# Two-row groups with 16-byte gaps for the input of a convolution stage, and transfers that begin at even rows

## The chip, the core and the metric

The kernel runs on one NeuronCore of one Trainium2 chip. Each compute engine (TensorE, called PE in the profile; VectorE, DVE; ScalarE, ACT; GpSimd, POOL) runs its own instruction stream in order. Transfers between memory and the on-chip buffer are issued from a further queue, SyncE (SP), and are carried out by 16 DMA engines that all issuers share. The metric is the time of one execution on the device in microseconds (us). Three runs of the kernel before gave 2673.44, 2696.38 and 2699.72 us, with a median of 2696.38.

## What is computed

The input `x` has 16 images of 16 channels of 256 x 256 float32 values. Two layers follow each other, each of the form "normalise in groups of two channels, convolve, add".

```python
def _gn(v, G=8, eps=1e-5):
    g = v.reshape(B_, G, C_ // G, H_, W_)
    m = jnp.mean(g, axis=(2, 3, 4), keepdims=True)
    s = jnp.var(g, axis=(2, 3, 4), keepdims=True)
    return ((g - m) / jnp.sqrt(s + eps)).reshape(v.shape)
# layer 0: a circular 3x3 convolution over 16 channels, written with FFTs
x = x + _L0_conv_ref(_gn(x), L0_conv_weight)
# layer 1: a Laplace-type spectral operator with poles and residues
x = x + _L1_conv_ref(_gn(x), L1_conv_ty, L1_conv_tx, L1_conv_weights_pole1,
                     L1_conv_weights_pole2, L1_conv_weights_residue)
```

Layer 0 needs the mean and the variance of every group of `x` before an image can be convolved. It is computed as a direct 3x3 convolution on PE. Layer 1 is computed with matrix products that stand for Fourier transforms.

## The kernel before

The program has four stages in time. The first (lines 100 to 701, from 0 to about 594 us) loads `x`, convolves it and stores the result `v` into the scratch tensors `vD`; beside this it builds tables for layer 1. The other three transform `v`, mix the channels per mode, and transform back. The change touches the first stage alone.

**How x lies.** The host prepares `x` as an array of shape (16 images, 128 partitions, 34 rows, 258 columns). A partition holds one channel and one of eight interleaved sets of rows, with a column of halo on either side, so a row is 258 x 4 = 1032 bytes and the 34 rows of a partition follow each other without a gap. Of the 34 rows, the first half-tile uses rows 0 to 17 and the second rows 16 to 33.

**How x is loaded.** A half-tile `xt` has 18 rows on 128 partitions; there are five buffers of them (line 109). `load_part` (line 122) issues one DMA for some of the rows of a half, and `PARTS` (line 120) cuts the 18 rows into 5, 4, 5 and 4. So a half takes four DMAs, an image eight, and the stage 128. A DMA of 5 rows moves one piece of 5160 bytes for each partition, a DMA of 4 rows one piece of 4128 bytes. All go through SP's queue. The eight DMAs of image 0 are issued first of all (line 131), then 12 constants, then image 1. From there `load_part` is called inside the main loop (line 686), for the image two ahead, at steps 4, 5, 10, 11 and 16, 17, 22, 23 of the 24 steps of an image.

**Who reads it.** DVE takes moments of row pairs of each half (`moments`, line 177): its call `j` reads rows 1+2j and 2+2j of the half. The calls for image b stand in the loop 36 to 29 steps ahead of its convolution for the first half, and from 21 to 18 steps ahead for the second. A handful of small operations then give the image's scaled weights `wc`. In `conv` (line 280) each of the 24 steps of an image issues 16 small matrix products, of 32 rows by 32 columns, which run on quarters of the PE array; each is recorded as two matmuls, with a weight load before each. So a step is 32 matmuls and 32 weight loads.

**What follows the product.** Every six steps a unit is complete. ACT moves four PSUM banks into the tiles `pair` (three buffers) and `far` (line 313); DVE adds the two and sums them (line 261); POOL subtracts (line 264); ACT squares for the statistics of layer 1 (line 272). Two DMAs of 512 KB then store `pair` into `vD` (line 323), in pieces of 2048 bytes, from SP's queue. A buffer of `pair` is free again when its store has landed. Table building (`make_hat`, `make_c`) puts further DMAs into SP's queue, among them 20 broadcasts `s_h<-hD` of 256 KB.

**What sets the order.** The stage is scheduled by hand (line 118): the loop at line 675 decides at which step each piece is issued, and each engine and queue runs its pieces in that order. At most eight of SP's DMAs are under way at a time, since SP's DMAs use eight semaphores in turn and a DMA waits until the last one on its semaphore has landed.

Of the kernel before, what the change touches and what calls it, by code (L numbers as in the profile page):

```python
# [18 lines left out]
N = 256  # L19
P = 128  # L20
# [4 lines left out]
def conv_then_laplace_kernel(ctx: ExitStack, tc: tile.TileContext, a: dict, out: bass.AP):  # L25
# [15 lines left out]
    nc = tc.nc  # L41
    x = a["x"]
# [66 lines left out]
    xp = p1.enter_context(tc.tile_pool(name="xt", bufs=5))  # L109
# [7 lines left out]
    psu = p1.enter_context(tc.tile_pool(name="p_setup", bufs=1, space=PSUM))  # L117
    p1.enter_context(tc.manual_schedule())

    PARTS = 0, 5, 9, 14, 18  # L120

    def load_part(t, b, h, i, j):
        nc.sync.dma_start(out=t[:, i:j], in_=x[b][:, 16 * h + i : 16 * h + j])

    def load_x(b, h):
        t = xp.tile([P, 18, N + 2], FP, name="xt", tag="xt")
        for i, j in zip(PARTS, PARTS[1:]):
            load_part(t, b, h, i, j)
        return t
# [545 lines left out]
    for g in range(24 * B + 3):  # L675
        conv(g)
        if g - 24 * (B - 4) in (16, 19, 22, 27, 30, 33):
            next(early, None)
        b, n = divmod(g, 24)
        if b + 2 < B and n % 12 in (4, 5, 10, 11):  # L680
            h, k = n // 12, (4, 5, 10, 11).index(n % 12)
            if k == 0:
                halves.setdefault(b + 2, []).append(
                    xp.tile([P, 18, N + 2], FP, name="xt", tag="xt")
                )
            load_part(halves[b + 2][h], b + 2, h, PARTS[k], PARTS[k + 1])
        for b, gen in at_step.get(g, ()):
            going.append([b, gen, next(gen)])
        for it in list(going):
            while it[2] is not None and g >= 24 * it[0] - it[2][0]:  # L690
                it[2][1]()
                it[2] = next(it[1], None)
            if it[2] is None:
                going.remove(it)
        run_jobs(g, slots.get(n, ()))
        next(tables, None)
# [31 lines left out]
    m, n = cols[:, 16:17], cols[:, 17:18]  # L728
# [136 lines left out]
    for u in range(len(units) + 1):  # L865
        at = units[u] if u < len(units) else None
        if at is not None:
            now = vq
            t = lp.tile([P, 2, 4, 3, P], FP, name="t", tag="t")
# [8 lines left out]
        if last is not None:  # L878
            i, b0 = last[:2]
# [9 lines left out]
        if last is not None:  # L889
            first_slots(b0, spec, *done)  # L890
            if b0 == B - 4:
                project(i, psd)
                (nc.sync if i + 1 < C else nc.scalar).dma_start(
                    out=aD[:, 2 * i : 2 * i + 2].rearrange("p r n -> p (r n)"),
                    in_=spec.rearrange("p r f b -> p (r f b)"),
# [504 lines left out]
    for n, (k, b0) in enumerate(units):  # L1400
# [13 lines left out]
        r = rp.tile([P, 4, 2, N], FP, name="r", tag="r")  # L1414
# [105 lines left out]
def _laid_out(x, L0_conv_weight, L1_conv_ty, L1_conv_tx, L1_conv_weights_pole1, L1_conv_weights_pole2, L1_conv_weights_residue):  # L1520

    g = {"ty": np.asarray(L1_conv_ty), "tx": np.asarray(L1_conv_tx)}
    x = np.asarray(x)
    xp = np.concatenate([x[..., -1:], x, x[..., :1]], -1)

    rows = 64 * np.arange(2)[:, None, None] + 2 * np.arange(33) - 1 + np.arange(2)[:, None]

    rows = np.concatenate([np.pad(rows, ((0, 0), (0, 0), (1, 0))), np.pad(N - 1 - rows, ((0, 0), (0, 0), (0, 1)))])
    g["x"] = xp[:, :, rows % N].transpose(0, 2, 3, 1, 4, 5).reshape(-1, P, 34, N + 2)
    w = np.asarray(L0_conv_weight)  # L1530
    band = np.zeros((4, 2, C, 2, 3, 2, C), w.dtype)
    for r in range(4):
        for j in range(2):
            for phase in range(2):
                for yo in range(2):

                    dy = (j - 1 - yo + 2 * phase) * (1 if r < 2 else -1)
                    if abs(dy) <= 1:
                        band[r, j, :, phase, :, yo, :] = w[:, :, 1 - dy, :].transpose(1, 2, 0)
    g["wband"] = band.reshape(P, 2, 3, 32)  # L1540

    def pairs(z):
        z = np.ascontiguousarray(z)
        return z.view(np.float32).reshape(z.shape + (2,))

    p1, p2, rs = (
        pairs(np.asarray(z))
        for z in (L1_conv_weights_pole1, L1_conv_weights_pole2, L1_conv_weights_residue)
    )

    g["poles"] = np.stack([p1.reshape(P, 8, 2), p2.reshape(P, 8, 2)], 1).transpose(0, 3, 1, 2).reshape(P, 2, 16)

    g["res_kq"] = np.repeat(rs.transpose(1, 3, 0, 2, 4).reshape(64, C, 4, 2), 2, 0)

    g["res_ip"] = np.repeat(rs.transpose(0, 2, 1, 3, 4).reshape(64, C, 4, 2), 2, 0)
    g["pole1_ip"] = np.repeat(p1.transpose(0, 2, 1, 3).reshape(64, C, 2), 2, 0)

    z = p2.reshape(4, 4, 8, 2, 4, 2).transpose(3, 1, 4, 0, 2, 5)
    z = np.broadcast_to(z[:, None, :, :, None], (2, 2, 4, 4, 2, 4, 8, 2))
    g["pole2_k"] = z.reshape(P, 32, 2)  # L1560

    e1 = p1.transpose(0, 2, 1, 3).reshape(4, 16, C, 2)
    g["pole_e1"] = np.stack([e1, e1], 1).reshape(P, C, 2)
    g["pole_e2"] = np.repeat(p2.transpose(0, 2, 1, 3).reshape(64, C, 2), 2, 0)
    return {n: np.ascontiguousarray(v) for n, v in g.items()}
# [17 lines left out]
```

## Time and profile before

| What | Value |
|---|---|
| median of three runs | 2696.38 us (2673.44 to 2699.72) |
| time of the profiled execution | 2673.52 us |
| its span, first to last instruction | 2671.8 us |
| mean granted TensorE clock | 0.980 |
| PE busy | 2494.0 us (93% of the span) |
| DVE busy | 1977.7 us (74%) |
| ACT busy | 1446.7 us (54%) |
| POOL busy | 1327.2 us (50%) |
| DMA traffic | 653.11 MB, mean 244 GB/s |

The span splits by stages as follows. The first row is the time until the first product of the convolution starts, and the second is the rest of the first stage.

| Stretch (us) | Length | PE busy | DVE busy | ACT busy | DMA share |
|---|---|---|---|---|---|
| 0 to 28.7 | 28.7 | 1.8 | 16.0 | 1.5 | 0.87 |
| 28.7 to 594 | 565.3 | 506.8 | 407.8 | 328.5 | 0.77 |
| 594 to 1245 | 651.0 | 625.1 | 540.7 | 381.2 | 0.57 |
| 1245 to 1910 | 665.0 | 622.4 | 510.2 | 414.0 | 0.74 |
| 1910 to 2671.8 | 761.8 | 737.9 | 503.0 | 321.5 | 0.81 |

"Busy" is the time in which an engine executed something. Matmuls are pipelined and their ends are modelled, so that a stretch of PE that looks busy may still run below PE's best rate. The DMA share is the mean over the 16 DMA engines of the time in which they carried a packet; a packet is one contiguous piece, and the records of the trace give its size, its start and its duration. "Issue" as a reason for a wait means that the engine waited for nothing that the profile shows.

### The profile page before, as it was taken

The page shows a single profiled execution, that of the slowest core. Times are in us where ns is not written, and L with a number is a line of the kernel's source. Part 1 is how long each engine was busy: PE and PEld are TensorE (multiplying, and loading weights), DVE is VectorE, ACT ScalarE, POOL GpSimd, SP SyncE. Part 2 cuts the span into 40 slices and gives each one's busy share as a digit, 9 for nine tenths or more (in the row PEclk, how much of TensorE's full clock was granted, in tenths as well). Part 3 has the DMA queues.
Part 4 walks back from the last instruction along what each step waited for, and adds up shares of the span by engine and source line. Part 5 has one row for each costly group of instructions (what it writes and reads, how often), then busy time and mean ns, then how long its engine had stood idle before and what let it go on. Part 6 is the DMA issues. An engine that isn't in the chain of part 4 may idle for free.

```text
span 2671.8 us, 83862 instructions
## 1 busy us (share of the span) xinstructions
PE 2494.0 (93%) x35314; PEld 1879.1 (70%) x35314; DVE 1977.7 (74%) x3805; ACT 1446.7 (54%) x2726; POOL 1327.2 (50%) x1180
## 2 busy tenths in 40 slices
PE   5988899888999999997999999999799999999998
PEld 2544454456777777774877888887688888888887
DVE  7767778738888888886877877887267666766666
ACT  2555666575666666664666666666344444444443
POOL 1333368432333333333366656676456566565653
PEclk9999999999999999997999999999899999999999
DMA  7787778855566556554777777777788888888884
GB/s 273 266 283 268 266 240 289 283 176 192 190 252 235 202 195 253 230 204 160 222 221 221 230 231 219 220 232 218 218 318 290 284 294 288 284 291 282 301 285 169
DMA packets 290871, 653.11 MB, mean 244 GB/s; under 512 B 44566, under 2 KB 159382, under 8 KB 280640
## 3 DMA queue, kind: packets, MB, share of 16 engines
q1 hardware_dynamic: 289456, 640.55, 71.1%
q8 instruction: 278, 4.55, 0.7%
q0 software_dynamic: 896, 3.02, 0.4%
q10 hardware_dynamic: 144, 4.19, 0.4%
q14 instruction: 97, 0.79, 0.1%
HBM read 368.15 MB, written 280.36 MB: 243 GB/s over the span
## 4 chain that ended last, share of the span: by engine, by line
PE 62%; DMA 5%; DVE 3%; SPq 3%; POOL 1%; ACT 1%; issue 1%; DVEq 0%; ACTq 0%; POOLq 0%
PE ps_mix L1096 9%; PE ps_y L764 9%; PE ps_p L1337 9%; PE ps_y L772 8%; PE ps_f L1361 8%; PE ps_f L1362 8%; PE ps_x L807 4%; DMA yD<-yt 4%; PE ps_s L1014 3%; PE ps_h L1321 2%; SPq L1110 2%; DVE sg L1030 2%; PE psd L792 1%; SPq L1083 1%; ACT yt L1209 1%
## 5 line engine op out<-in xcount | busy, mean ns | idle before, releaser
L1096 PE MATMUL ps_mix<-abd,sg 128*64 128x128 f32 x8192 | 484.3, 276 | 35.2 <-ACT yt L1209 22.2
L1096 PEld LDWEIGHTS ps_mix<-abd,sg 128*64 128x64 f32 x8192 | 450.5, 138 | 91.8 <-ACT yt L1209 49.6
L294 PE MATMUL ps_conv<-xt,wc 32*32 32x512 f32 x12288 | 451.9, 615 | 55.6 <-issue 49.2
L1301 POOL TENSOR_TENSOR u<-yk 128x512 f32<-128x512 f32 (+1 forms) x268 | 353.2, 1351 | 281.1 <-PE ps_p L1337 215.6
L294 PEld LDWEIGHTS ps_conv<-xt,wc 32*32 32x32 f32 x12288 | 251.2, 104 | 246.2 <-issue 163.5
L780 ACT ACTIVATE t<-ps_y,vmr 128x384 f32<-128x384 f32 x512 | 297.0, 580 | 163.8 <-PE ps_y L772 163.6
L1030 DVE STREAM_SHUFFLE sg<-ps_s 128x512 f32<-128x512 f32 (+1 forms) x264 | 326.1, 1325 | 0.0
L764 PE MATMUL ps_y<-tabE,vq 128*128 128x256 f32 x1024 | 313.1, 388 | 13.7 <-DVE vq L753 12.2
L264 POOL TENSOR_TENSOR pair<-pair,far 128x1024 f32<-128x1024 f32 x64 | 151.6, 2368 | 343.2 <-DVE pair L261 308.7
L772 PE MATMUL ps_y<-tabO,vq 128*128 128x256 f32 x1024 | 305.8, 380 | 0.0
L1361 PE MATMUL ps_f<-pt,inv 128*128 128x256 f32 x1008 | 300.5, 380 | 0.0
L1362 PE MATMUL ps_f<-hs,ey 128*128 128x256 f32 x1008 | 299.8, 379 | 0.0
L1337 PEld LDWEIGHTS ps_p<-inv,u 128*128 128x128 f32 x2048 | 266.2, 193 | 47.7 <-issue 25.5
L1365 DVE TENSOR_TENSOR r<-ps_f,q 128x256 f32<-128x256 f32 x256 | 107.0, 418 | 253.1 <-ACT q L1364 253.1
L1337 PE MATMUL ps_p<-inv,u 128*128 128x128 f32 x2048 | 279.4, 280 | 10.8 <-POOL u L1305 10.7
L1209 ACT COPY yt<-ps_mix 128x512 f32<-128x512 f32 x352 | 191.6, 593 | 151.0 <-DMA yD<-yt 104.7
L764 PEld LDWEIGHTS ps_y<-tabE,vq 128*128 128x128 f32 x1024 | 189.4, 191 | 90.5 <-ACT q L820 50.3
L1364 ACT COPY q<-ps_f 128x256 f32<-128x256 f32 x256 | 95.4, 373 | 286.0 <-PE ps_f L1362 283.3
L752 POOL TENSOR_TENSOR vq<-vf 128x512 f32<-128x512 f32 x64 | 81.4, 1272 | 294.5 <-DVE vf L756 277.5
L1339 ACT COPY pt<-ps_p 128x512 f32<-128x512 f32 x256 | 150.1, 586 | 134.5 <-PE ps_p L1337 130.2
L772 PEld LDWEIGHTS ps_y<-tabO,vq 128*128 128x128 f32 x1024 | 195.4, 191 | 26.8
L1029 ACT ACTIVATE sg<-ps_s,mcol 128x512 f32<-128x512 f32 (+1 forms) x264 | 167.5, 688 | 82.4 <-PE ps_s L1014 82.2
(240 smaller groups left out, 4056.1 us busy)
## 6 DMA issues: line engine op xcount, KB each, us to landing
vD<-pair SPq DMA_DIRECT2D x128, 512.0 KB
yD<-yt SPq DMA_DIRECT2D x512, 128.0 KB
vl<-vD SPq DMA_DIRECT2D x128, 512.0 KB
out_y<-ol SPq DMA_DIRECT2D x128, 512.0 KB
s<-vD SPq DMA_DIRECT2D x126, 512.0 KB
aD<-spec SPq DMA_DIRECT2D x15, 4096.0 KB
yk<-yD SPq DMA_DIRECT2D x60, 1024.0 KB
xt<-in_x SPq DMA_DIRECT2D x64, 645.0 KB
```

The source lines that it names most:

```text
L294: nc.tensor.matmul(acc[r][32 * c : 32 * c + 32], lhsT=ready[b][0][rows, phase, tap], rhs=halves[b][u // 2][rows, q : q + 5 : 4, 2 - tap : ...
L764: nc.tensor.matmul(ps[:, 0:N], lhsT=vf[:, xo, 0, j], rhs=tabE[:, 0 : i + 2 : i + 1], start=True, stop=False, skip_group_check=True,)
L772: nc.tensor.matmul(ps[:, P : P + N], lhsT=vf[:, xo, 1, j], rhs=tabO[:, i : C + 1 : C - i], start=False, stop=True, skip_group_check=True,)
L780: nc.scalar.activation(t[:, xo, j].rearrange("p l n -> p (l n)"), ps[:, 0:384], AF.Copy, scale=vmr[:, 0, b0 + j, i : i + 1],)
L1029: nc.scalar.activation(to[..., k : k + 2], src, AF.Copy, scale=nsgn)
L1030: nc.vector.stream_shuffle(to[..., C + k : C + k + 2], src, swap)
L1096: nc.tensor.matmul(ps[64 * t : 64 * t + 64, j], lhsT=sg[:, f : f + 2].rearrange("p f m -> p (f m)"), rhs=abd[jq][:, :, 2 * t + cc, 2 * jj ...
L1209: (nc.vector.tensor_copy if m >= (2 if late else 3) else nc.scalar.copy)(o, src)
L1301: nc.gpsimd.tensor_tensor(u[:, :, j].rearrange("p b (c n) -> p c b n", c=8), in0, in1, o)
L1337: nc.tensor.matmul(ps[:, at], lhsT=u[:, n], rhs=tab, start=True, stop=True)
L1361: nc.tensor.matmul(ps[:, e], lhsT=tab, rhs=pt[:, e], start=True, stop=False)
L1362: nc.tensor.matmul(ps[:, e], lhsT=ey[:, e], rhs=hs, start=False, stop=True)
```

## The change

The host puts the 34 rows of a partition into 17 groups of two rows, 2064 bytes each, and adds four float32 values (16 bytes) behind each group. `load_part` reads 2064 of every 2080 bytes. In the on-chip tile the rows stay where they were, without gaps. Since a transfer now consists of whole groups, its first row must be even, and the 18 rows are cut into 4, 6, 4 and 4 instead of 5, 4, 5 and 4. The number of DMAs, their places in the loop and the bytes that they move are the same; all that computes is unchanged.

```diff
-    PARTS = 0, 5, 9, 14, 18
+    PARTS = 0, 4, 10, 14, 18
 
     def load_part(t, b, h, i, j):
-        nc.sync.dma_start(out=t[:, i:j], in_=x[b][:, 16 * h + i : 16 * h + j])
+        nc.sync.dma_start(
+            out=t[:, i:j].rearrange("p (n r) x -> p n (r x)", r=2),
+            in_=x[b][:, 8 * h + i // 2 : 8 * h + j // 2, 0 : 2 * (N + 2)],
+        )
...
-    g["x"] = xp[:, :, rows % N].transpose(0, 2, 3, 1, 4, 5).reshape(-1, P, 34, N + 2)
+    xr = xp[:, :, rows % N].transpose(0, 2, 3, 1, 4, 5).reshape(-1, P, 17, 2 * (N + 2))
+    g["x"] = np.pad(xr, ((0, 0), (0, 0), (0, 0), (0, 4)))
```

## The prediction

> **What bounds the kernel now.** Only the first stage, 0 to 594 us of 2671.8, loads `x`, so I read that stage. The idle times of PE in it came first (who waited for whom: time in total, times, longest):
>
> ```profile
> PE ps_conv L294 <- issue: 49.2, 34, 2.8
> PE ps_stat L160 <- DVE wsum L158: 16.2, 1, 16.2
> PE ps_stat L207 <- DVE xe L200: 7.7, 3, 6.6
> PE ps_conv L294 <- DVE wc L237: 4.1, 1, 4.1
> ```
>
> The last three are the start, before 28.7 us. The first is the steady state: 34 pauses for no reason that the profile shows. The timeline of PE places some (start, length, engine, line, count, idle time before):
>
> ```profile
> 55.41 1.48 PE L294 MATMUL ps_conv<-xt,wc 32*32 32x512 f32 x29
> 59.12 4.67 PE L294 MATMUL ps_conv<-xt,wc 32*32 32x512 f32 x127 [2.23 <-issue]
> 66.08 2.35 PE L294 MATMUL ps_conv<-xt,wc 32*32 32x512 f32 x66 [2.29 <-issue]
> ```
>
> The two pauses stand 127 matmuls and as many weight loads apart, about 256 PE instructions, and so do nearly all others: the index of the PE instruction after a pause leaves the same remainder by 256. The DMA view of 28.7 to 594 us tells what comes in such blocks:
>
> ```profile
> DMA packets 60618, 145.56 MB, mean 257 GB/s; under 512 B 6599, under 2 KB 11207, under 8 KB 60499
> q1 hardware_dynamic: 60499, 143.78, 75.3%
> q8 instruction: 99, 1.62, 1.2%
> ```
>
> Queue q8 brings 99 packets of 16384 bytes while PE runs some 25,000 instructions: one packet for each 256, 64 bytes an instruction. So PE's instructions come through the same 16 DMA engines as `x` (q1), and PE pauses when a block is late. I set each q8 packet against the block boundary before it. With DMA idle a packet starts 1.05 to 1.15 us behind the boundary, takes about 1.0 us, and PE enters the next block no sooner than 1.25 us after it has landed. Such blocks take 3.8 to 4.0 us. Behind data the packet starts up to 4.5 us late, and the block takes 5.9 to 7 us. In 51 of 98 blocks the boundary follows the landing within 1.7 us: there the fetch ends last, also where no pause shows.
>
> **How long a fetch waits** decides this case. On a busy DMA engine each packet starts as the one before ends, so I chained packets back from a fetch to 1.05 us behind its boundary. In the deepest queues the chain is: 7 of 4128 B and 7 of 5160 (63.5 KB), 16 of 2048 and 8 of 4128 (64.3), 12 of 4128 and 5 of 2048 with one of 5160 (63.4), 33 of 2048 (66.0), and in the second stage 2 of 32768 (64). The counts go from 2 to 36 while the bytes stay near 64 KB: a fetch waits for bytes, not for a number of packets.
>
> **The change, part by part.** Packets: before 64 x 128 = 8192 of 5160 B and as many of 4128 B; after, 9 pairs x 128 x 32 halves = 36864 of 2064 B. Prices without contention are the median durations of packets in the trace: 5160 B 199 ns, 4128 B 160, 2048 B 84, 1024 B 46. Between 2048 and 4128, 2064 B comes to 84.6 ns. The first load of `x`, alone on the engines, confirms the level (3 to 13 us):
>
> ```profile
> DMA packets 1000, 4.15 MB, mean 415 GB/s; under 512 B 112, under 2 KB 112, under 8 KB 1000
> q1 hardware_dynamic: 1000, 4.15, 102.1%
> ```
>
> Less 112 packets of 4 B at 9 ns, that is 162 us of engine time for 888 packets of 4.67 KB, 183 ns each, halfway between 160 and 199. Sum: before 8192 x (199 + 160) / 16 = 183.8 us for each engine; after 36864 x 84.6 / 16 = 194.9 us. So x costs 11 us more DMA time, 0.7 us an image.
>
> Bounds. The means under load in this stage are 252.7 (5160 B), 169.1 (4128 B) and 98.5 ns (2048 B). By them x costs 216.0 us before and, at 99, 228 after: +12. From below: half of a loaded 4128-byte packet, 84.6 ns, gives 195, which is -21 us. Not absurd, since much of the excess of 5160 B sits in the first packet of a transfer (424 ns on average for the first 16 of 128) and behind a fetch (554 ns, against 445 for 4128 B and 231 for 2048 B): a shorter packet restarts sooner. From above: 2048-byte packets take about 120 ns where the broadcasts run beside them, which gives 276, +60. I take +11; nearest are the 2048-byte rows.
>
> What lies on the path:
> - The start. DVE waits for `wband` at 15.04 us behind the eight transfers of image 0, and PE's start at 28.7 follows from that. On each engine these are 8 packets a transfer: 4 x 8 x (199 + 160) ns = 11.5 us before, 18 groups x 8 x 84.6 ns = 12.2 us after: +0.7 us, all on the path.
> - The fetch wait. 64 KB are 2.53 us in packets of 5160 B (12.7 x 199) and 2.69 in packets of 2064 B (31.75 x 84.6), +0.16; x is 53% of the bytes (76 of 143.8 MB) and 51 blocks are bound by the fetch: 0.16 x 0.53 x 51 = 4.3 us.
> - The longer queue. Stores of `pair` wait behind x (ACT waits for them 8.1 us in all), DVE for x some 17 us after the start, and more fetches find data ahead. Of 11 us between none and all pass through; I take half, 5.5.
> - The cuts. `moments` call 1 reads rows 3 and 4, hitherto both in the first transfer; now row 4 comes with the second, of 6 rows, 24 x 84.6 ns = 2.0 us after the first, less the 0.68 us of call 0. That shows only where call 0 had to wait for x at all: three times after the start, 0.5 to 1.9 us, all in the last images. At most 3 x 1.3 us, and I take 1. Behind it on DVE stand the addition of line 261 and the next weights. Call 6 read rows of two transfers already; calls 1 and 4 are new, 64 more semaphore waits of some 20 ns on a DVE that is 72% busy, free.
> - SP. A DMA of 256 pieces (`vD`) takes SP 0.36 us at least, one of 128 (`x`) 0.33. Some 0.05 us x 128 = 6 us of a queue that waits 201 us for POOL's `pair`: free; without that cover, the `vD` stores behind would come 0.05 us later each. Their count and places in the loop stay.
>
> Sum: 0.7 + 4.3 + 5.5 + 1 = 11.5 us. The profiled execution took 2673.5 us, so 2685 after. Of the three runs one lies at that level and two 25 us higher, for which the page shows no cause; by the median it would be 2708. I put the time between the levels, at 2697.
>
> **Two rules weighed.** The row: PE pauses 49.2 us at block boundaries. The Trainium skill (Runtime: NRT & Kernel Launch, "Instruction fetch mechanics") has blocks of 256 instructions too, but calls crossing them mostly hidden. By it the 4.3 us would go, and 7 us remain. The second row: 4096-byte packets, from rows of whole KB, take 159 ns and 4128-byte ones from odd places 160, so an odd start costs at most 1 ns. The Trainium skill (DMA: Bandwidth & Descriptors, "How a descriptor splits into AXI transactions") lets a start off a 256-byte boundary cost extra 32-byte beats, on average some 3.5 on the 65 of a group. By it, as an estimate, 2064 B would cost 5% more, another 10 us of DMA time: against the change.
>
> **The rivals.**
> - Slower: short packets dear under load. Place: the queue of q1 while broadcasts or stores run, where 2048-byte packets rise from 84 to 120 ns. Price: at 120, +60 us of DMA time, half on the path, with the other terms +36 us: 2710 to 2735 by level. It decides from about +42 us of DMA time, that is a loaded mean of 112 ns. For it: the 95th percentile of 2048 B is 180 ns. Against it: the stage's mean is 98.5, broadcasts included. 0.18.
> - Faster: a fetch waits for a count of packets after all, or the cheaper restart counts. With some 16 packets ahead, those of x would last 1.35 us instead of 2.5 to 2.9; 1.3 x 0.53 x 51 = -35 us, with the other terms about -28: 2645 to 2669. For it: in the third stage, with packets of 1024 B, fetches start only 0.3 to 1.6 us behind the boundary. Against it: the chains above; that queue is merely shorter in bytes. 0.13.
> - The pieces are not 2064 B but single rows of 1032 B: 73728 x 46.3 / 16 = 213 us, +30 of DMA time, half of it on the path, with the other terms +21: 2695 to 2717. Nothing speaks for it, as both sides are contiguous over a group. 0.02.
> - The forecast: -5 to +25 us, within 1%: 0.67.
>
> **How the numbers follow.** One per cent, 27 us, is about what a measurement of this kernel can tell from no change. The forecast's own range over both levels is 2668 to 2722. Until a fifth is left out it reaches into the rivals: 2652 to 2732. Slower by over 1%: the slow rival 0.18 and 0.03 of the forecast's tail, 0.21. Faster: the fast rival 0.13 less 0.01 that stays inside. Same: 0.67.
>
> **What would show it.** In the profile after: packets of q1 up by some 20,500; the median of 2064 B at 84 to 86 ns; `wband` landing near 15.7 us and PE's start near 29.4; pauses of PE at 256 instructions still there, 45 to 60 us; chains ahead of a fetch at 64 KB, now of some 30 packets; the first stage's end at 600 to 610 us; the later stages unchanged. Pauses below 30 us would make the byte window wrong; a loaded mean above 112 ns would make the price wrong.

## The result, and the profile after

| | Before | After |
|---|---|---|
| median of 20 runs each | 2693.1 us (2673.44 to 2702.97) | 2687.21 us (2676.3 to 2700.42) |
| ratio after / before | | 0.9986, 95% interval 0.9968 to 1.0003 |
| profiled execution, its span | 2673.52, 2671.8 us | 2679.25, 2677.5 us |
| mean granted clock | 0.980 | 0.980 |

By the ratio the change is worth -3.8 us, with an interval from -8.6 to +0.8: it holds no change as well, and lies within 1%. Ratios here and below leave out runs that took over 1.5% longer than the fastest of their kernel; among these 40 there are none. The two profiled executions lie the other way round, 5.7 us apart. Executions of one kernel differ by up to 30 us, so one pair of traces can't settle a sign of this size, and what follows uses traces for counts, durations and waits, and medians of several runs for times.

The pages show first what was done to the transfers (the whole program; packets, bytes, share of the 16 engines' span). Before:

```profile
q1 hardware_dynamic: 289456, 640.55, 71.1%
```

After:

```profile
DMA packets 311352, 653.11 MB, mean 244 GB/s; under 512 B 44567, under 2 KB 159383, under 8 KB 301121
...
q1 hardware_dynamic: 309936, 640.55, 71.5%
```

Queue q1 carries 20,480 packets more, and the bytes are equal: 36,864 pieces of 2064 B stand where 16,384 of 4128 and 5160 B were. That disposes of the rival in which the pieces are single rows. In the records the median of a 2064 B packet is 85 ns and its mean 97.9 ns, beside 99.5 for those of 2048 B, the stores and broadcasts. Over the stage `x` costs 36864 x 97.9 / 16 = 225.6 us of time on each DMA engine, 9.6 more than the 216.0 of before.

VectorE's timeline at the start (start, length, engine, line, operation, tiles, count, idle time before), first before:

```profile
15.04 0.47 DVE L155 TENSOR_REDUCE wsum<-wband 128x32 f32<-128x192 f32 x1 [4.78 <-DMA wband<-in_wband]
```

Then after:

```profile
15.81 0.47 DVE L158 TENSOR_REDUCE wsum<-wband 128x32 f32<-128x192 f32 x1 [4.88 <-DMA wband<-in_wband]
16.32 0.18 DVE L159 TENSOR_SCALAR wsum<-wsum 128x32 f32<-128x32 f32 x1
16.54 0.35 DVE L161 COPY wsum<-wsum 128x32 f32<-128x32 f32 x3
```

`wband` lands behind image 0 and lets VectorE begin at 15.81 us, against 15.04 before. TensorE's first product of the convolution follows at 29.47 instead of 28.71 us: +0.76. Its waits from 0 to 620 us (who waited for whom: time in total, times, longest):

```profile
PE ps_conv L297 <- issue: 49.4, 31, 4.5
PE ps_stat L163 <- DVE wsum L161: 16.9, 1, 16.9
...
PE ps_stat L210 <- DVE xe L203: 9.8, 3, 6.6
PE ps_conv L297 <- DVE wc L240: 4.1, 1, 4.1
```

The pauses of the steady state are where they were, 49.4 us for 49.2. The DMA view of 28.7 to 600 us and VectorE's wait for `x` in the same stretch, before:

```profile
q1 hardware_dynamic: 60956, 144.67, 75.0%
```

```profile
DVE xst L179 <- DMA xt<-in_x: 17.7, 10, 6.0
```

And after:

```profile
q1 hardware_dynamic: 79051, 144.63, 77.0%
q8 instruction: 99, 1.62, 1.2%
```

```profile
DVE xst L182 <- DMA xt<-in_x: 19.3, 6, 5.8
```

The DMA share of q1 rises from 75.0 to 77.0%, and VectorE's waits for `x` go from 17.7 us in 10 to 19.3 in 6. I summed by how much each of 96 instruction packets starts behind its block's boundary: 247 us before, 247 after. So `x` comes in 2.25 times as many packets, DMA time grows by what the packets' durations say, and neither the fetches nor the pauses show it.

After the convolution nothing differs beyond the scatter: from the first `ps_y` of the second stage to the end it is 2064.8 us before (607.0 to 2671.8) and 2067.7 after (609.8 to 2677.5).

### The profile page after: what moved, and what is told of

It is laid out like the page before. It is cut to its first block, busy times and chain, and to the rows that moved or that the text cites. A ratio compares the mean times of both kernels' runs of the same rounds, so it can differ in the third digit from the quotient of the medians.

```text
span 2677.5 us, 83893 instructions
## 1 busy us (share of the span) xinstructions
PE 2495.3 (93%) x35314; PEld 1881.3 (70%) x35314; DVE 1977.4 (74%) x3805; ACT 1446.7 (54%) x2726; POOL 1326.1 (50%) x1180
## 4 chain that ended last, share of the span: by engine, by line
PE 61%; DMA 5%; SPq 4%; DVE 3%; ACT 2%; issue 1%; POOL 1%; ACTq 0%; DVEq 0%; POOLq 0%
PE ps_mix L1099 9%; PE ps_y L767 9%; PE ps_p L1340 9%; PE ps_y L775 8%; PE ps_f L1364 8%; PE ps_f L1365 8%; DMA yD<-yt 5%; PE ps_x L810 4%; SPq L1113 2%; PE ps_s L1017 2%; PE ps_h L1324 2%; PE psd L795 1%; ACT yt L1212 1%; DVE sg L1033 1%; SPq L1086 1%
## 5 line engine op out<-in xcount | busy, mean ns | idle before, releaser
L297 PE MATMUL ps_conv<-xt,wc 32*32 32x512 f32 x12288 | 451.8, 614 | 57.0 <-issue 49.4
```

The source lines that it names most:

```text
L297: nc.tensor.matmul(acc[r][32 * c : 32 * c + 32], lhsT=ready[b][0][rows, phase, tap], rhs=halves[b][u // 2][rows, q : q + 5 : 4, 2 - tap : ...
```

## Experiments

Two terms of the prediction ask for a test: that extra DMA time delays the stage (half of it, I said), and that a fetch waits for what lies ahead of it in the queue, in bytes. To see them above the scatter I ran the first stage alone, which is 23% of the time. All kernels named s_ have this edit, which leaves out stages two to four:

```diff
+    nc.sync.dma_start(out=out[0, 0, :, 0, 0, 0:P], in_=ones)
     p1.close()
+    ptab.close()
+    return
```

The ratio is that of the stage to the whole kernel before on the same chip, so 0.001 is 2.7 us. "Stretch" is the time from the convolution's first product to its last; "delays" is the sum over 96 instruction packets defined above; "DMA idle" is the share of 30 to 590 us with fewer than three of the 16 engines busy. These three, and the time of the first product, are worked out from the records of the one profiled execution. How a block's boundary is set moves a sum of delays by up to 18 us, so smaller differences of it are not read. Where values are missing, that execution was the slowest of its kernel (s_cuts, s_before_r) or they were not worked out.

| Kernel | median (runs) | ratio and interval | first product | stretch | delays | DMA idle |
|---|---|---|---|---|---|---|
| s_before | 617.23 (5) | 0.2298 (0.2287 to 0.2308) | 28.93 | 574.1 | 253 | 0.20 |
| s_after | 613.61 (4) | 0.2279 (0.2270 to 0.2287) | 29.34 | 571.5 | 256 | 0.19 |
| s_rows | 618.50 (5) | 0.2299 (0.2291 to 0.2306) | 30.80 | 573.6 | 248 | 0.16 |
| s_half | 624.24 (6) | 0.2310 (0.2300 to 0.2320) | 33.41 | 571.2 | 253 | 0.105 |
| s_cuts | 615.49 (5) | 0.2272 (0.2258 to 0.2285) | 28.96 | | | |
| s_rows2 | 616.64 (5) | 0.2289 (0.2278 to 0.2300) | 30.65 | 576.4 | 269 | 0.17 |
| s_lite | 593.07 (4) | 0.2202 (0.2192 to 0.2211) | 29.46 | 550.5 | 206 | 0.35 |
| s_fine | 590.10 (4) | 0.2192 (0.2183 to 0.2201) | 29.23 | 552.7 | 206 | 0.25 |
| s_before_r | 615.96 (6) | 0.2276 (0.2265 to 0.2287) | | | | |
| s_after_r | 611.44 (5) | 0.2267 (0.2257 to 0.2276) | 29.39 | 567.6 | 272 | 0.19 |
| s_cuts_r | 611.59 (5) | 0.2275 (0.2265 to 0.2285) | 28.84 | 564.3 | | |

The first four ran together on one chip, s_cuts, s_rows2 and s_lite on a second, the rest on a third. The same kernel's ratio moves by up to 0.0022 from chip to chip (s_before and s_before_r), so differences are best taken within a group.

**The two ends: s_before and s_after.** No edit but the one above.

> The kernel before, ended after its first stage (the other three stages are left out; one tile is stored to the output). It is the yardstick for the three that follow, since the spread of the later stages falls away. The profiled execution of the whole kernel had its last store of the first stage issued at 600 us and landed a few us later, so 603 to 608 us. Both theories expect the same here.

> The changed kernel, ended after its first stage. Theory A, the prediction's: half of the 11 us of DMA time that shorter packets cost comes onto the path, 4 us of longer waits for instruction blocks and 0.7 us at the start besides: +11 us against s_before. Theory B: x is loaded two images ahead, so what its packets cost stays hidden and only the start shows: 0 to +2 us. Theory C: shorter packets restart sooner behind a fetch or a store and pay their cost back: -8 to 0 us.

The stage alone repeats the whole kernel's result: -0.0019 here and -0.0009 in the repeat, -5.1 and -2.4 us, each with an interval of some 4 us to either side, where the whole kernel has -3.8. Theory A's +11 us is out. The time lies in the range of theory C, but not for its reason: the shorter packets do not pay their cost back, since `x` takes some 10 us more of each DMA engine. About 1.5 us of either gain can be the granted clock, which is 0.0025 higher on average over the runs of s_after and of s_after_r than over those of s_before and s_before_r. The delays and the idle share of the DMA engines stay within what two executions of one kernel differ by (s_after and s_after_r: 256 and 272).

**More DMA time for the same bytes: s_rows and s_half.** Both keep the old cuts of 5, 4, 5 and 4 rows. s_rows has 16 bytes behind every row, so the pieces are 1032 B; s_half has 12 bytes behind every half row, 516 B.

```diff
# s_rows, against before
+        nc.sync.dma_start(out=t[:, i:j], in_=x[b][:, 16 * h + i : 16 * h + j, 0 : N + 2])
+    g["x"] = np.pad(g["x"], ((0, 0), (0, 0), (0, 0), (0, 4)))
# s_half, against before
+            out=t[:, i:j].rearrange("p n (r x) -> p (n r) x", r=2),
+            in_=x[b][:, 32 * h + 2 * i : 32 * h + 2 * j, 0 : N // 2 + 1],
...
+    g["x"] = np.pad(xr, ((0, 0), (0, 0), (0, 0), (0, 3)))
```

> The first stage with the old row cuts and 16 bytes behind every row, so pieces of 1032 bytes: 73728 packets at 46.3 ns, 213 us of DMA time for each engine against 184. Theory A: half of +29.5, that is 15, and 64 KB ahead of a fetch take 2.94 us instead of 2.53, 0.41 x 0.53 x 51 = 11 us, and +1.8 us at the start: +28 us. Theory B: +2 to +4 us. Theory C: below +15 us, and the mean of the packets under load lies closer to the uncontended 46 ns than that of 5160 bytes (253 against 199).

> The first stage with the old row cuts and pieces of half a row, 516 bytes with 12 bytes between them: 147456 packets at 28.2 ns, 260 us of DMA time for each engine against 184. Theory A: half of +76, that is 38, 1.05 x 0.53 x 51 = 28 us of waits for instruction blocks, and +4.7 us at the start: +71 us. Theory B: +5 to +10 us until the queue is full all the time; x and the stores would then take 31 of the 35 us of an image. Theory C: less than half of A.

The DMA views of 31 to 590 us, s_before, then s_rows, then s_half:

```profile
DMA packets 59302, 142.60 MB, mean 255 GB/s; under 512 B 6509, under 2 KB 11091, under 8 KB 59187
...
q1 hardware_dynamic: 59187, 140.88, 75.0%
```

```profile
DMA packets 110818, 143.93 MB, mean 257 GB/s; under 512 B 6549, under 2 KB 76954, under 8 KB 110703
...
q1 hardware_dynamic: 110703, 142.21, 80.3%
```

```profile
DMA packets 179082, 145.18 MB, mean 260 GB/s; under 512 B 6581, under 2 KB 145223, under 8 KB 178967
...
q1 hardware_dynamic: 178967, 143.46, 90.3%
```

The bytes stay within 2% and the engines are occupied for 75, 80 and 90% of the time. From 0 to 605 us q1 holds each engine for 452.6, 482.7 and 541.1 us, 30 and 88 more than before. The convolution as a whole does not follow: its stretch is 574.1, 573.6 and 571.2 us, where two executions of one kernel differ by 4 (s_after and s_after_r). What moves is the start, by 1.9 and 4.5 us, since nothing runs beside the load of image 0. By the ratios the stage is 0.3 and 3.2 us slower, give or take 4 us, which the start covers. Half of the extra DMA time would have been 15 and 44 us, so theory A's +28 and +71 are out; theory B's +2 to +4 and +5 to +10 are nearest. Theory C's mark is there in part: the 1032 B packets take 53.3 ns on average, 13% over their 47, where those of 5160 B take 27% over theirs. Their time still grows by 30 us.

Most of the time goes where the idle share shows it: 0.20, 0.16, 0.105. The engines that run longer do so in time in which they stood. In s_rows the waits stay near those of s_before. In s_half they do not, but what they gain and lose cancels (waits by engine, 29.5 to 600 us; s_before first, then s_half):

```profile
PE ps_conv L294 <- issue: 56.1, 34, 4.8
PE ps_stat L207 <- DVE xe L200: 1.1, 1, 1.1
```

```profile
DVE xst L179 <- DMA xt<-in_x: 18.1, 6, 6.6
```

```profile
PE ps_conv L297 <- issue: 43.7, 38, 2.5
PE ps_stat L210 <- DVE xe L203: 10.6, 5, 4.4
```

```profile
DVE xst L182 <- DMA xt<-in_x: 23.8, 11, 6.2
```

VectorE waits 5.7 us more for `x`, and TensorE 9.5 us more for `xe`, which VectorE makes from the moments of an image. One of these five waits, 4.4 us, is at image 1 just behind the start; the other four, 6.2 us, come each some 5.5 us after VectorE stood for `x`. So part of the extra DMA time does reach TensorE here. The pauses at block boundaries are 12.4 us shorter at the same time, and the sum is no worse.

The chains ahead of a fetch, followed as in the prediction, correct its byte window at one end. A packet's record does not name its DMA engine, so the links are made by times alone, and with short packets several fit. In the changed kernel the deepest are 15 of 2064 B with 16 of 2048 (62.2 KB), 22 with 11 (66.3) and 23 with 11 (68.4), 32 to 37 packets with the 4 B ones: still some 64 KB, as forecast. In s_half many end after 69 to 71 packets of 516 B, 34.8 KB and 1.8 us, others after 98 to 110, 49 to 55 KB. So for small packets a count, or the depth of what is queued, seems to end the window before 64 KB. Which of the two was not tried. The delays say the same without chains: 64 KB in 516 B packets would take 1.05 us more than before, yet the delay that one fetch in ten exceeds falls from 4.6 us in s_before to 3.9 in s_half.

**The cuts alone, and the gaps alone: s_cuts and s_rows2.** s_cuts has the new cuts and the old contiguous layout (pieces of 4128 and 6192 B); s_rows2 has the new cuts with the pieces of s_rows.

```diff
# s_cuts, against before; s_rows2 has this line and the two of s_rows
+    PARTS = 0, 4, 10, 14, 18
```

> The first stage with the new row cuts 4, 6, 4, 4 alone; x lies as before, so pieces of 4128 and 6192 bytes and the DMA time of before. s_after had 0.0019 less of the whole kernel's time than s_before (0.2279 against 0.2298), 5 us, though its packets cost 10 us more DMA time. If the cuts give that gain, this kernel has a ratio of 0.2275 to 0.2285, about 4 us below s_before; if the shorter packets give it, 0.2293 to 0.2303, as s_before; if it is chance, also as s_before.

> The first stage with the new row cuts and pieces of one row, 1032 bytes. Against s_rows (ratio 0.2299) only the cuts differ. If the cuts give the gain of s_after: 0.2280 to 0.2286, 4 us less than s_rows. If pieces of 2064 bytes give it: 0.2295 to 0.2303, no change from s_rows.

s_cuts, at 0.2272, ran on another chip than s_before and decides nothing. Within the third chip s_cuts_r stands 0.0001 below s_before_r by ratio and 4.4 us below it by median, so the two measures disagree. s_rows2 is 0.0010 below s_rows, on another chip, at 0.2289 between its two forecasts. These differences are no larger than the intervals. The cuts cost nothing that can be seen; whether the few microseconds between s_before and s_after come from them or from the packets stays open.

**Fewer bytes, and then the DMA time put back: s_lite and s_fine.** From image 3 on, each transfer of s_lite moves the first two rows of its part only, and the moments and products read rows that were moved, as many of them as before. s_fine moves the same two rows in 12 pieces of 172 B, from a second copy of `x`. So s_fine has the bytes of s_lite and, nearly, the DMA time of the changed kernel.

```diff
# both: what is read
+            r0 = 1 + 2 * (j % 8) if b < 3 else PARTS[j % 8 // 2]
+                if b > 2:
+                    q = 10 * (u % 2) + q % 2
# s_lite: what is moved
+        if b > 2:
+            j = i + 2
# s_fine: what is moved
+        if b > 2:
+            g0 = 8 * h + i // 2
+            nc.sync.dma_start(
+                out=t[:, i : i + 2].rearrange("p r (k x) -> p (r k) x", k=6),
+                in_=a["xf"][b][:, 12 * g0 : 12 * g0 + 12, 0:43],
+            )
```

> The changed kernel's first stage, in which each transfer of x from image 3 on moves its first two rows only; the moments and the products of those images read these rows again in place of the others, at the same sizes and counts (the output is then that of other data). It takes 20 of 36 rows from 13 of 16 images: 13 x 8 x 10 groups x 84.6 ns = 88 us of DMA time for each engine, a sixth of all the stage's traffic time. If x's transfers are hidden (theory B): the ratio of s_after, 0.2279, within 0.001. If the stage hangs on waits for instruction blocks behind data: x falls from 53% to a third of the bytes, the waits of 2.9 us behind a boundary fall toward the 1.05 us of an idle queue, some 0.8 us for each of about 50 blocks: 40 us less, a ratio of 0.213. If half of the DMA time passes: 44 us less.

> As s_lite (from image 3 on two rows of a part are moved, and read in place of the others), but these rows come in 12 pieces of 172 bytes from a second copy of x. By the packets of 128 and 256 bytes (12.7 and 18.4 ns) a piece costs some 14.7 ns, so x takes 8 x 8 x 12 x 14.7 ns = 11.3 us of each engine's time an image: nearly the 12.2 us of s_after, with the 44% of bytes of s_lite. If s_lite was 20 us faster because the DMA engines were less busy, this one is at s_after's ratio, 0.2279, 613 us. If it was faster because fewer bytes stand ahead of PE's instruction blocks, this one is at s_lite's, 0.2202, 593 us.

q1 from 31 to 590 us in s_after, s_lite and s_fine:

```profile
q1 hardware_dynamic: 77563, 141.75, 77.5%
```

```profile
q1 hardware_dynamic: 62997, 111.18, 60.9%
```

```profile
q1 hardware_dynamic: 209044, 110.66, 74.4%
```

Thirty megabytes less make the stage 20.7 us faster by the ratios of s_lite and s_after, and 20.2 by those of s_fine and s_after_r, which ran on one chip (0.2192 and 0.2267). That is half of what either theory of s_lite with a gain said, 40 and 44 us. The granted clock does not make it: up to the convolution's end it withheld 17.1 us of full speed in s_lite and in s_fine, 20.5 in s_after and 13.7 in s_after_r (each record's length times one less the granted share). The DMA engines of s_fine are occupied for 74.4% of the time, nearly as long as those of s_after; that takes nothing of the gain back, as the second forecast of s_fine had it. So the gain does not go with the time for which the DMA engines are busy. It goes with the bytes: the sum of the delays falls from 256 to 206 in both, and the pauses follow (waits of TensorE, 29.5 to 600 us, s_after, s_lite, s_fine):

```profile
PE ps_conv L297 <- issue: 47.1, 29, 3.8
```

```profile
PE ps_conv L301 <- issue: 37.0, 24, 4.5
```

```profile
PE ps_conv L306 <- issue: 30.0, 22, 4.8
```

Ten to 17 of the 20 us are in these pauses. Other causes run beside them: VectorE waits for `xt` for 14.2 and 11.9 us instead of 18.6, and small pieces may also shorten the window ahead of a fetch. So the experiment shows that bytes matter where DMA time does not, and that the delays fall with them; how much of the gain is the delays' is not separated.

**Repeats.** s_before_r, s_after_r and s_cuts_r are the three kernels again, beside s_fine.

> s_before again, beside the next two: the three first-stage times lie 2 to 4 us apart, as much as their runs spread. If the cuts or the packets gain 4 us, it is again 4 us above s_after_r; if that was chance, they lie within 2 us.

> s_after again. If the gain is real: 4 us below s_before_r. If chance: within 2 us of it. By the prediction's terms it would be 11 us above.

> s_cuts again. If the row cuts give what gain there is: within 1.5 us of s_after_r. If the pieces of 2064 bytes give it: within 1.5 us of s_before_r.

The order of s_before and s_after comes out a second time, 2.4 us apart by ratio, between the 4 us and the 2 us of the forecasts, and s_cuts_r lies between them by ratio. A real gain and chance are not told apart.

**The same bytes at other times: f_spread.** This is the whole changed kernel with other steps for its loads: of each four, the first comes one step later, the second two later, and the third two earlier.

```diff
-        if b + 2 < B and n % 12 in (4, 5, 10, 11):
-            h, k = n // 12, (4, 5, 10, 11).index(n % 12)
+        if b + 2 < B and n % 12 in (5, 7, 8, 11):
+            h, k = n // 12, (5, 7, 8, 11).index(n % 12)
```

> The whole changed kernel, with the transfers of x at other steps of the convolution's loop: at steps 5, 7, 8 and 11 of each twelve in place of 4, 5, 10 and 11. The stores of vD fall at steps 3 and 4 of every six, so the changed kernel has four transfers within three neighbouring steps and none in the next three. Theory 1, PE's instruction blocks wait for the bytes that stand queued ahead of them, and bunched transfers make that queue long: the sum of the fetch delays in the first stage falls below 235 us (247 in the changed kernel), its pauses below 45 us, and the time is 5 to 10 us below the changed kernel's, a ratio to the kernel before of 0.995 to 0.997. Theory 2, the bytes in all count and not when they are sent: the delays stay at 245 to 275 us and the ratio at 0.997 to 1.000. Theory 3, the later transfers come too late for the moments: VectorE's waits for xt after the start rise above 25 us (19.3 in the changed kernel), and the ratio is above 1.000.

The median is 2676.25 us (8 runs) beside 2691.16 for the kernel before (13 runs), a ratio of 0.9933, interval 0.9910 to 0.9955. Relative to the changed kernel that is 0.9933 / 0.9986 = 0.9947, some 14 us, with 7 to 22 as the interval. It beats both kernels, by more than any theory said (the interval just reaches the first one's 0.995), and not by the first theory's way. VectorE's waits for `x` from 28.7 to 600 us and TensorE's pauses:

```profile
DVE xst L182 <- DMA xt<-in_x: 10.5, 4, 3.9
```

```profile
PE ps_conv L297 <- issue: 46.5, 35, 3.7
PE ps_conv L297 <- DVE wc L240: 4.1, 1, 4.1
PE ps_conv L297 <- ACT pair L316: 1.8, 1, 1.8
```

The delays sum up to 257 us, no less than the 247 of the changed kernel, and the pauses lose only 2.9 us. So the first theory's reason falls with its gain standing; the second theory had the delays right and the time wrong. The third had the sign wrong: VectorE waits less for `x`, 10.5 us for 19.3. The records point to one transfer. In the changed kernel 14.1 of the 19.3 us stand before the moments of rows 9 and 10 of a second half (images 4, 6 and 8), and row 10 comes with the third of the four transfers, the one that f_spread issues two steps earlier. In f_spread VectorE no longer waits there; its 10.5 us all stand before rows 13 and 14, and row 14 comes with the fourth. By the profiled executions the convolution ends at 583.9 instead of 597.6 us, 13.7 earlier, and 8.8 of it remain at the program's end. The granted clock is part of that: up to the convolution's end the clock withheld 8.5 us of full speed here and 13.7 in the changed kernel, so at most 5 us. TensorE's own account agrees: of the 13.7 us, 5.1 are shorter matmuls, 4.7 shorter pauses and 3.1 shorter waits for other engines; the pauses differ as much between two executions of one kernel (47.1 and 52.3 in s_after and s_after_r). Over all runs the mean granted clock is 0.9795 here, 0.9766 in the kernel before on this chip and 0.9778 in the changed kernel, so up to 8 of the 18 us against the kernel before, and 5 of the 14, can be the clock. What carries the rest, the 8.8 us of VectorE's waits or something else, no run separates: open.

## Why the prediction came out right, and where its steps did not

The forecast was 2697 us, from 2652 to 2732, most likely within 1%. The measured 2687.21 and the class agree, but two of its four terms did not pass what I let them pass. That they failed did not show in the class, since all of them together were half of one per cent. That the point is within 10 us is in part luck: the two levels that I saw in three runs are not there in 20, of which 17 lie between 2687 and 2703, and from their median of 2693.1 the same sum would give 2705.

- **What the change does to the transfers** held: 20,480 more packets, 85 ns for a forecast 84.6, and +9.6 us of DMA time under load for +12. The rival in which short packets are dear decides at a loaded mean of 112 ns; it is 97.9.
- **The start, +0.7 us**, held: `wband` at 15.8 for 15.7, the first product at 29.47 for 29.4. In the stage alone it is +0.4, and the two kernels with more DMA time scale it to +1.9 and +4.5. It is the only place where the DMA time of this change is seen on the path.
- **The longer queue, +5.5 us**, is the step that failed. "Of 11 us between none and all pass through; I take half": the share is about none. s_rows adds 30 us of DMA time and s_half 88, and their stretches are 0.5 and 2.9 us shorter than that of s_before. In s_half some of it passes, 9.5 us of waits for `xe`, and shorter pauses hide it. The row that I should have weighed was in front of me: a DMA share of 0.77 leaves idle time in which a queue of the same bytes can run longer.
- **The fetch wait, +4.3 us**, failed as well. The bytes ahead of a fetch in the deepest queues are 62 to 68 KB, about as forecast, but the sum of the delays is 247 us in both kernels. A longer queue is not seen to add its 0.16 us to every block that a fetch ends last. The share of `x` was also too high: 76 MB is all of `x`, but the 143.8 MB are those of a window with 110 of its 128 transfers, 65 MB, so 45% and 3.7 us by the same sum. And from one execution to the next the sum moves by more (256 and 272 in the two profiles of s_after).
- **The cuts, +1 us**: VectorE's waits for `x` rise by 1.6 us in the traces, and the wait of call 1 for row 4 is there at image 0, 1.3 us. In other profiles of the same cuts the waits are 17.1 (s_after_r) and 12.6 (s_cuts_r), so nothing of this size can be read from one trace.
- **The sum, +11.5 us**, should have been about +1; measured is -3.8 with an interval to +0.8. A small gain, if it is one, remains that no term had; its place stays open.
- **The rivals.** The faster one, a wait for a count of packets, falls for packets of 2 KB and more, with chains of 32 to 37 packets instead of 16; for 516 B there are signs of a count. It would have given -28 us.
- **The marks that I named.** Pauses at 45 to 60 us: 49.4. First stage's end at 600 to 610: the last product is at 597.6 and the last store of `vD` is issued at 603.6. Later stages: +2.9 us of 2065, unchanged within the scatter.

Of the two rules weighed, neither gives a better sum. The Trainium skill (Runtime: NRT & Kernel Launch, "Instruction fetch mechanics") has crossings mostly hidden. The sum without the 4.3 us is nearer to the result, but not for the page's reason: TensorE pauses 49.4 us at crossings here. By the Trainium skill (DMA: Bandwidth & Descriptors, "How a descriptor splits into AXI transactions"), the odd starts should, as an estimate, cost 5%; the 2064 B packet has a median of 85 ns where the 2048 B one has 84, so no run here shows such a cost.

## What to carry to other kernels

Ask of extra DMA time where it can go before you price it: where the queue drains now and then (here a fifth of the stage), 30 us more of it for the same bytes cost nothing that these runs resolve, and only a load that everything waits for, such as that of the first image, pays in full. An unchanged total can also hide two changes, as the longer waits and shorter pauses of s_half do. Bytes, and perhaps the moment at which they are sent, are another matter: 30 MB less were worth 20 us, and other steps for the same transfers some 14, of which the clock can be 5. A forecast made of small terms of one sign is worth a test of the largest term's share before it is added up.

## What the runs showed of the hardware

The median time of a packet of `x` follows one line over the sizes seen, about 9 ns + 37 ns for each 1000 bytes: 28 ns for 516 B, 47 for 1032, 85 for 2064, 160 for 4128, 199 for 5160. Even pieces of 172 B took 16.5 ns on average under load. And DMA engines that were occupied for 90% of the time by small packets held TensorE up no more in sum than at 75%, with 253 us of delays in both: pauses of 43.7 us in place of 56.1, and waits for `xe` of 10.6 in place of 1.1.
